# The last product of a two-layer graph kernel: four steps product by product, and eight blocks without their scale

## Chip, cores and metric

The kernel runs on one core of one Trainium2 chip. The metric is the device time of one execution in microseconds (us). All data is float32.

## What is computed

```python
def _L0_gnn_ref(cur, incidence_m):            # layer 0
    head = (incidence_m > 0).astype(float32)
    head = head / max(norm of each row of head, 1e-12)
    inc = incidence_m + head
    return (inc @ cur) / sum of each row of inc

def _L1_gnn_ref(X, A, W):                     # layer 1
    A2 = A + eye(4096)
    dscale = diagonal(A2) ** -0.5
    temp = A2 @ X @ W.T
    return relu((dscale[:, None] * A2 * dscale[None, :]) @ temp)

x = layernorm(x + _L0_gnn_ref(x, adj))        # called x1 here
x = layernorm(x + _L1_gnn_ref(x, adj, W))     # eps = 1e-5
```

x is 4096x512, adj 4096x4096, W 512x512. Row block b is rows 128b to 128b+127; there are 32. The end of the kernel computes, for each block, `layernorm(x1 + relu(dscale * C))`, where C is the block's result of the last big product and dscale one number for each row.

## The kernel before, in words

Layer 0 comes first and leaves x1 in device memory, one buffer for each row block (`x1_rows`). Then two big products follow, called k = 2 (A2 @ x1) and k = 3 (A2 @ temp, scaled). Both use a two-level scheme of seven products in place of eight. The outer level has seven products p, in the order given by `ORDER`; for k = 3 the last one is p = 4. Each outer product is done in two halves s of the columns. For each half and p there are eight steps kk = 0 to 7, and in each step the inner level makes seven matmuls, one into each of seven PSUM banks, named q1, q2, q6, q5, q7, q3, q4 (banks 0 to 6, `acc`). A matmul in float32 is two instructions on TensorE. The eighth bank, 7, is the `spare()` one, which transposes go through.

The results are kept transposed: features on the partitions, rows along the free axis, in four tiles c11, c12, c21, c22 of four feature parts each. After the eight steps of an outer product, `inner` combines the seven banks (L682 to L692) and `outer` adds the result into these tiles.

The program is written out by hand in one order[...]. The main loop (L993) goes through the steps n. In step n it first loads and prepares on VectorE (DVE) what step n + 2 needs: `prepare` calls `add_up` (L166), three additions that make the four operand sums `s` (called S3, S1, S2 and S4) of a step, and `sum_b` (L253) makes the sums `ts` of two steps of the other operand. The matmuls of q6, q5, q7 and q3 read these sums; q1, q2 and q4 don't read `s`. Then come the step's seven matmuls (`multiply2`, L278), and what the queue of finished row blocks asks for.

A row block that is finished is taken up by `layer1` (L859): its four feature parts are transposed back through bank 7 (`turn_back`, L844), ScalarE (ACT) rectifies and scales it in one operation out of PSUM (`rectify`, L848), and a part `rest`, run one step later, adds x1 on DVE (L695), takes the statistics (L149, L151), has ScalarE take the root (L153), and normalises on ScalarE (L162); the store is issued from GpSimd (POOL, L873). The block's x1 rows are fetched by `fetch` (L857), a DMA issued from POOL's queue, which stands behind POOL's earlier instructions.

In the last outer product (k = 3, p = 4, the second half) there are three such ordinary blocks left and then eight blocks whose first half of features isn't ready before the very end. These eight are taken up in pairs, four items, by `layer1_first` (L876): their second half of features, complete by then, is transposed into bank 7, rectified by two ScalarE operations, and x1 is added on POOL (L887). The items come at these places: two ordinary blocks in step kk = 1, the third and the first pair in kk = 2, the second and third pair in kk = 3, the fourth pair in kk = 4, after its matmuls.

The last steps, `TAIL` of them (three: kk = 5, 6, 7), are not multiplied in the loop but in `finish` (L895), product by product: all q1, then all q2, and so on, so that the combination of the banks can run beside the matmuls. After q7 four blocks are transposed, rectified (ScalarE) and added to x1 (POOL, L922), after q4 the other four; `measure` takes the statistics, and `leave` normalises on ScalarE or DVE and stores from SP's queue (L942).

Three buffers in turn hold the sums `s` (L241), so a step's sums can be made only when the matmuls of three steps before are over.

Of the kernel before, what the change touches and what calls it, by code (L numbers as in the profile page):

```python
# [8 lines left out]
F32 = mybir.dt.float32  # L9
BF16 = mybir.dt.bfloat16  # L10
AF = mybir.ActivationFunctionType
ALU = mybir.AluOpType

P = 128
LN_EPS = 1e-5
# [11 lines left out]
def tile_adj_resnorm_d2(  # L27
# [37 lines left out]
    nc = tc.nc  # L65
    N, D = x.shape
    H = D // 2
    NB = N // P
    NP = NB // 2
# [8 lines left out]
    SW = 512  # L78
    NS = NQ * P // SW
    SB = SW // P  # L80
# [7 lines left out]
    work = ctx.enter_context(tc.tile_pool(name="work", bufs=2))  # L88
    rows = ctx.enter_context(tc.tile_pool(name="rows", bufs=1))

    def bank(m):

        return psum.tile([P, D], F32, tag=f"q{m}", name=f"q{m}")

    def spare():
        return bank(7)

    def row_tile(tag, bufs, shape=(P, D)):
        return rows.tile(list(shape), F32, tag=tag, name=tag, bufs=bufs)


    ident = const.tile([P, P], F32, name="ident")
    make_identity(nc, ident)
    eps_t = const.tile([P, 1], F32, name="eps_t")
# [7 lines left out]
    dscale = const.tile([P, NB], F32, name="dscale")  # L112
# [3 lines left out]
    x1_rows = [dram.tile([P, D], F32, name=f"x1_{b}") for b in range(NB)]  # L116
# [39 lines left out]
    def normalise(y, mv, sd):  # L156

        rs = small.tile([P, 1], F32, name="rs")
        nc.vector.reciprocal(rs, sd)
        nb = small.tile([P, 1], F32, name="nb")  # L160
        nc.vector.scalar_tensor_tensor(nb, mv[:, 0:1], -1.0, rs, op0=ALU.mult, op1=ALU.mult)
        nc.scalar.activation(y, y, AF.Identity, scale=rs, bias=nb)  # L162
# [11 lines left out]
        nc.vector.tensor_add(pair, pair, ident.unsqueeze(1).to_broadcast([P, 2, P]))  # L174


    TAIL = 3
    LA = 2
    ORDER = {2: (4, 5, 1, 6, 7, 2, 3), 3: (2, 3, 5, 1, 6, 7, 4)}

# [8 lines left out]
    steps = [(k, s, p, kk) for k in (2, 3) for s in range(NS) for p in ORDER[k] for kk in range(NQ)]  # L189
    groups = [st[:3] + (st[3] // 2,) for st in steps[::2]]  # L190
    pools = {}
# [35 lines left out]

    def prepare(n):
        k, s, p, kk = steps[n]
        for i in range(n, len(steps) if n == len(steps) - TAIL else n + 1):  # L230
            complete(i)
        a = loaded.pop(n, None)
        r = resident[kk] if k == 2 and p != 4 and p != 7 else None
        if k == 2 and p in (3, 6):
            if a is not None:
                nc.vector.tensor_add(r, r, a)
            nc.gpsimd.dma_start(out=outer_2[s, kk, S2 if p == 6 else S4], in_=r)
            a = r
        i = made["s"]
        made["s"] += 1  # L240
        sm = (work, pools["work"], work)[i % 3].tile([P, 4, SW], F32, tag="s", name="s")  # L241
        add_up(sm, a)
        if k == 2 and p in (1, 2) and kk < EARLY:
            raises.append(lambda: nc.vector.tensor_add(r, r, a))
        ready[n] = a, sm
# [55 lines left out]
    chunks, sums, slots, counts, scale, natural = {}, {}, {}, {}, {}, {}  # L301
# [186 lines left out]
    def take(h, acc):  # L488

        y = row_tile("z", 2)  # L490
        nc.scalar.copy(y[:, 0:H], acc[0][:, 0:H])
        nc.scalar.copy(y[:, H:D], acc[1][:, 0:H])
        nc.scalar.copy(deg0[:, h:h + 1], acc[0][:, H:H + 1])
        return y
# [199 lines left out]
    def add(o, y):  # L694
        nc.vector.tensor_add(o, o, y)  # L695
# [145 lines left out]
    def turn_back(ps, at, h, r, cols, fs):  # L841

        for i, d in enumerate(2 * f + e for f in fs for e in range(2)):
            nc.tensor.transpose(ps[:, at + i * P:at + (i + 1) * P], C_of[3][h][d // 2][:, 2 * r + d % 2, cols], ident)  # L844

    def rectify(o, ps, b):

        nc.scalar.activation(o, ps, AF.Relu, scale=dscale[:, b:b + 1])  # L848

    def fetch(kind, h, *items):  # L850

        for j, _, _ in items:
            b = j + h * NP
            if b not in late:
                own = kind is layer1_first
                late[b] = late["pool"].tile([P, D], F32, tag=f"y{b}" if own else "y", name="y", bufs=1 if own else 3)
                nc.gpsimd.dma_start(out=late[b], in_=x1_rows[b])  # L857

    def layer1(h, item):  # L859

# [14 lines left out]

    def layer1_first(h, *items):  # L876

        ps = spare()
        for i, (j, r, cols) in enumerate(items):
            turn_back(ps, i * H, h, r, cols, (1,))  # L880
        for i, (j, r, cols) in enumerate(items):
            b = j + h * NP
            o = late["pool"].tile([P, D], F32, name=f"o{b}")
            st = late["pool"].tile([P, 2, 6], F32, name=f"st{b}")
            rectify(o[:, H:D], ps[:, i * H:(i + 1) * H], b)
            y, late[b] = late[b], (late[b], o, st)
            nc.gpsimd.tensor_add(o[:, H:D], o[:, H:D], y[:, H:D])  # L887

        def rest():
            for j, _, _ in items:  # L890
                _, o, st = late[j + h * NP]
                nc.vector.bn_stats(st[:, 1, :], o[:, H:D])
        later.append(rest)

    def finish(h, items, acc):  # L895


        c21 = C_of[3][h][0]
        q1, q2, q6, q5, q7, q3, q4 = range(7)
        p1, p5, u2, u3 = (row_tile(t, 1) for t in ("p1", "p5", "u2", "u3"))  # L900
        w2 = row_tile("t", 1, (P, 4, H))[:, 0:2, :].rearrange("p a d -> p (a d)")
        tail = [(steps[n][3], factors(n)) for n in range(len(steps) - TAIL, len(steps))]
        stats = {}

        def multiply(m):
            for kk, f in tail:
                right, left = f[m]
                nc.tensor.matmul(acc[m], left, right, start=False, stop=(kk == NQ - 1))  # L908

        def put(i, op):  # L910
            y = row_tile("y", 2)
            op(y)
            nc.vector.tensor_sub(c21[:, i, :], y, c21[:, i, :])

        def turn(t):
            j, r, cols = items[t]
            b = j + h * NP
            ps = bank((t + 7) % 8)
            turn_back(ps, 0, h, r, cols, (0,))
            y, o, _ = late[b]  # L920
            rectify(o[:, 0:H], ps[:, 0:H], b)
            nc.gpsimd.tensor_add(o[:, 0:H], o[:, 0:H], y[:, 0:H])  # L922

        def measure(t):
            b = items[t][0] + h * NP
            _, o, st = late[b]
            nc.vector.bn_stats(st[:, 0, :], o[:, 0:H])
            mv = late["pool"].tile([P, 2], F32, name=f"mv{b}")
            nc.vector.bn_aggr(mv, st)
            sd = late["pool"].tile([P, 1], F32, name=f"sd{b}")  # L930
            nc.scalar.activation(sd, mv[:, 1:2], AF.Sqrt, bias=eps_t)
            stats[b] = mv, sd

        def leave(t, by_act):
            b = items[t][0] + h * NP
            o, (mv, sd) = late[b][1], stats[b]
            if by_act:
                normalise(o, mv, sd)
            else:
                nc.vector.reciprocal(sd, sd)  # L940
                nc.vector.tensor_scalar(o, o, mv[:, 0:1], sd, op0=ALU.subtract, op1=ALU.mult)
            nc.sync.dma_start(out=out[b * P:(b + 1) * P, :], in_=o)  # L942

        multiply(q1)
        nc.scalar.copy(p1, acc[q1])
        multiply(q2)
        put(0, lambda o: nc.vector.tensor_add(o, acc[q2], p1))
        multiply(q6)
        nc.vector.tensor_add(u2, acc[q6], p1)
        multiply(q5)  # L950
        nc.scalar.copy(p5, acc[q5])
        nc.vector.tensor_add(w2, u2, p5)
        multiply(q3)
        put(1, lambda o: nc.vector.tensor_add(o, acc[q3], w2))
        multiply(q7)
        for t in range(4):
            turn(t)
        nc.vector.tensor_add(u3, acc[q7], u2)
        put(3, lambda o: nc.vector.scalar_tensor_tensor(o, u3, -1.0, p5, op0=ALU.mult, op1=ALU.subtract))
        multiply(q4)  # L960
        measure(0)
        measure(1)
        put(2, lambda o: nc.vector.tensor_sub(o, acc[q4], u3))
        for t in range(4, 8):
            turn(t)
        measure(2)
        measure(3)
        leave(0, True)
        leave(1, False)
        leave(2, True)  # L970
        measure(4)
        leave(3, False)
        measure(5)
        leave(4, True)
        measure(6)
        leave(5, True)
        measure(7)
        leave(6, True)
        leave(7, False)

    def take_up(item):
        kind, args = item
# [10 lines left out]
    for n, (k, s, p, kk) in enumerate(steps):  # L993
# [59 lines left out]
        if n + 1 == len(steps) // 2:  # L1053

            scope.close()
            ring3 = ctx.enter_context(tc.tile_pool(name="ring3", bufs=2))
            late["pool"] = ctx.enter_context(tc.tile_pool(name="late", bufs=1))
            i = made["a"] % 4
            pools["turn"] = [ring3] * 2 + pools["turn"][i:] + pools["turn"][:i]
            made["a"] = 0  # L1060
            PF = 3
# [36 lines left out]
```

## Time and profile before

| What | Value |
|---|---|
| Time, median of three runs | 2283.88 us (2283.74 to 2288.45) |
| The profiled execution's own time | 2284.03 us |
| Its span in the profile | 2282.1 us |
| Granted TensorE clock, mean | 0.998 |
| TensorE matmul busy | 2255.1 us, 99% |
| DVE busy | 1854.4 us, 81% |
| ScalarE busy | 417.3 us, 18% |
| GpSimd busy | 383.3 us, 17% |
| DMA | 555.8 MB, mean 244 GB/s |

In the profile's lines, L12 is line 12 of the kernel before. PE is TensorE's matmuls, PEld its weight loads, DVE VectorE, ACT ScalarE, POOL GpSimd, SP SyncE; a q behind an engine is its sequencer, which issues DMAs. A line such as "2239.33 0.56 POOL L873 ... [1.18 <-ACT o L162]" gives the start, the duration, the engine, the source line, the operation with output and input, the number of instructions, and in brackets how long the engine was idle before and what ended it. Times count from the start of the span.

### The profile page before, as it was taken

To read this page: it belongs to the slowest core of one execution; us is meant where nothing else is said; L and a number is where in the kernel's file an instruction comes from. 1 tells how busy PE (TensorE), PEld (TensorE's weight loads), DVE (VectorE), ACT (ScalarE), POOL (GpSimd) and SP (SyncE) were. 2 spreads that over 40 slices of the span, in tenths; PEclk is the share of its full clock that TensorE was granted. 3 is DMA by queue.
4 is the path that set the end of the run, shared out by engine and by line. 5 is a ranking of instruction groups with operands and counts; after the bars stand their busy time and mean duration, and the time that the engine had idled before them with its cause. 6 is when DMAs were issued, how large, how long until landed. Compare 5 with 4: busy or idle time off the path is not lost.

```text
span 2282.1 us, 22004 instructions
## 1 busy us (share of the span) xinstructions
PE 2255.1 (99%) x7359; PEld 1380.3 (60%) x7359; DVE 1854.4 (81%) x2619; ACT 417.3 (18%) x991; POOL 383.3 (17%) x548
## 2 busy tenths in 40 slices
PE   8999999999999999999999999999999999999997
PEld 6888888888888844444555444555544444444443
DVE  6988988988988777788876778887666788776788
ACT  4333223332232000000222100122110011100013
POOL 0111112211111110001333300232320000100013
PEclk9999999999999999999999999999999999999999
DMA  9788777878777576575767857576785676766573
GB/s 330 274 287 262 260 233 270 272 262 270 238 240 239 187 266 259 198 283 184 270 240 227 262 209 271 191 283 261 209 256 218 220 258 241 253 238 227 209 269 117
DMA packets 155936, 555.80 MB, mean 244 GB/s; under 512 B 17920, under 2 KB 32272, under 8 KB 117424
## 3 DMA queue, kind: packets, MB, share of 16 engines
q1 hardware_dynamic: 114624, 417.38, 51.6%
q0 software_dynamic: 41200, 137.03, 18.2%
q8 instruction: 58, 0.95, 0.2%
q14 instruction: 54, 0.44, 0.1%
HBM read 434.78 MB, written 119.55 MB: 243 GB/s over the span
## 4 chain that ended last, share of the span: by engine, by line
PE 89%; DVE 5%; DMA 3%; ACT 2%; issue 1%; POOL 0%; SPq 0%; DVEq 0%; ACTq 0%
PE q L278 55%; PE q L472 27%; PE q L766 3%; PE q L485 2%; DMA nat<-adj 2%; DVE s L167 1%; PE q L908 1%; PE q L844 1%; DVE s L169 0%; ACT z L816 0%; ACT nat L332 0%; DVE a L442 0%; DVE mask L435 0%; ACT t L816 0%; DVE ts L257 0%
## 5 line engine op out<-in xcount | busy, mean ns | idle before, releaser
L278 PE MATMUL q<-s,ts 128*128 128x512 f32 x1326 | 612.2, 592 | 0.1
L472 PE MATMUL q<-b,s 128*128 128x256 f32 (+1 forms) x1920 | 454.4, 379 | 0.0
L278 PEld LDWEIGHTS q<-s,ts 128*128 128x128 f32 x1326 | 251.6, 190 | 299.1 <-issue 268.3
L167 DVE TENSOR_TENSOR s<-a 128x1024 f32<-128x1024 f32 x236 | 290.2, 1230 | 161.4 <-PE q L278 131.3
L472 PEld LDWEIGHTS q<-b,s 128*128 128x128 f32 x1920 | 363.1, 189 | 53.1 <-DVE z L510 0.5
L472 PE MATMUL q<-b,a 128*128 128x258 f32 (+1 forms) x1440 | 352.5, 380 | 0.7 <-ACT p L503 0.6
L278 PE MATMUL q<-a,tr 128*128 128x512 f32 x692 | 329.4, 592 | 1.8 <-DMA a<-adj_r 1.8
L472 PEld LDWEIGHTS q<-b,a 128*128 128x128 f32 x1440 | 272.5, 189 | 40.9 <-ACT p L503 1.5
L278 PE MATMUL q<-s,tr 128*128 128x512 f32 x442 | 225.7, 592 | 0.0
L278 PEld LDWEIGHTS q<-a,tr 128*128 128x128 f32 x692 | 129.5, 190 | 145.1 <-issue 138.9
L332 ACT ACTIVATE nat<-nat,tiny 128x512 f32<-128x512 f32 x240 | 170.9, 714 | 235.9 <-DMA nat<-adj 235.7
L278 PE MATMUL q<-a,ts 128*128 128x512 f32 x346 | 176.8, 592 | 0.0
L169 DVE TENSOR_TENSOR s<-a,s 128x512 f32<-128x512 f32 x236 | 167.7, 711 | 8.1
L170 DVE TENSOR_TENSOR s<-a,s 128x512 f32<-128x512 f32 x236 | 167.3, 709 | 8.0
L442 DVE TENSOR_TENSOR a<-a,mask 128x1024 f32<-128x1024 f32 x123 | 150.7, 1225 | 6.6 <-DVE mask L435 0.5
L435 DVE SCALAR_TENSOR_TENSOR mask<-a,sc 128x1024 f32<-128x1024 f32 (+2 forms) x129 | 154.1, 1196 | 2.1
L278 PEld LDWEIGHTS q<-s,tr 128*128 128x128 f32 x442 | 84.0, 190 | 92.1 <-issue 84.6
L684 ACT COPY p<-q 128x512 f32<-128x512 f32 x27 | 15.6, 577 | 631.5 <-PE q L278 631.5
L278 PEld LDWEIGHTS q<-a,ts 128*128 128x128 f32 x346 | 65.7, 190 | 83.0 <-issue 76.1
L425 POOL DMA_DIRECT2D oa<-sr x64 | 57.7, 902 | 283.8 <-DVE sr L416 181.6
L873 POOL DMA_DIRECT2D out<-o x24 | 13.1, 547 | 507.8 <-ACT o L162 507.8
L278 PE MATMUL q<-r,tr 128*128 128x512 f32 x192 | 92.7, 593 | 0.0
(193 smaller groups left out, 2129.4 us busy)
## 6 DMA issues: line engine op xcount, KB each, us to landing
a<-adj_r SPq DMA_DIRECT2D x112, 1024.0 KB, 6.6
a<-oa SPq DMA_DIRECT2D x80, 1024.0 KB, 5.3
nat<-adj SPq DMA_DIRECT2D x240, 256.0 KB, 7.4
a<-adj_q SPq DMA_DIRECT2D x60, 1024.0 KB, 6.2
tr<-ob SPq DMA_DIRECT2D x112, 512.0 KB, 4.0
oa<-sr POOLq DMA_DIRECT2D x64, 512.0 KB, 7.2
oa<-r POOLq DMA_DIRECT2D x32, 1024.0 KB, 9.2
y<-x POOLq DMA_DIRECT2D x64, 256.0 KB, 7.2
```

Of the source, the lines that this page charges most:

```text
L167: nc.vector.tensor_add(s[:, S3:S1 + 1, :], a[:, A11:A22 + 1, :], a[:, A21, :].unsqueeze(1).to_broadcast([P, 2, w]))
L169: nc.vector.tensor_add(s[:, S2, :], a[:, A11, :], s[:, S1, :])
L170: nc.vector.tensor_add(s[:, S4, :], a[:, A12, :], s[:, S2, :])
L278: nc.tensor.matmul(acc[m], left, right, start=(kk == 0), stop=(kk == NQ - 1))
L332: nc.scalar.activation(y, a, AF.Sign, bias=tiny, scale=2.0 ** 64, accum_out=accum)
L425: nc.gpsimd.dma_start(out=dst, in_=sr.rearrange("p m (k i) -> p (m k) i", i=P))
L435: nc.vector.scalar_tensor_tensor(m, v, 0.0, s.unsqueeze(1).to_broadcast(list(v.shape)), op0=ALU.is_gt, op1=ALU.mult)
L442: nc.vector.tensor_add(z, z, y)
L472: nc.tensor.matmul(acc[m][:, 0:w], left, b[:, right, 0:w], start=(kk == 0), stop=(kk == NP - 1))
L485: nc.tensor.matmul(y[:, 0:w], left, slots[kk][:, op, 0:w], start=(kk == 0 and left is k1), stop=(kk == NP - 1 and left is k2))
L766: nc.tensor.matmul(ps, left[:, e, :], wt[:, right, e, :], start=(e == 0), stop=(e == 1))
L844: nc.tensor.transpose(ps[:, at + i * P:at + (i + 1) * P], C_of[3][h][d // 2][:, 2 * r + d % 2, cols], ident)
```

## The change

1. `TAIL` is four instead of three: step kk = 4 is no longer multiplied in the loop, but with the last three in `finish`, product by product. The places of the four items of `layer1_first` in the loop stay, so the third and the fourth pair's transposes now follow each other on TensorE with no matmul in between. The sums of the last two steps go into c11 and c12, which are free by then.
2. The last eight blocks are not scaled by dscale. Since layernorm takes out a common factor of a row, x1 is divided by dscale instead (`root` is 1/dscale), and eps by its square (`eps_by`). The division of x1 is done on ScalarE in `layer1_first`, directly after the rectification; DVE's addition of x1 follows one step later. POOL's additions are gone. A pair of blocks shares one tile, and one ScalarE operation rectifies both.
3. In `finish`, one DVE operation rectifies two blocks out of PSUM and adds x1 (`take`). The eight blocks are in two groups of four, r = 0 and 1. For r = 1 a quarter of the features is done ahead of the last q4 product, so that only the quarter from c21's third part is left after it; that part is finished in two halves. Root, reciprocal and offset are taken for up to four blocks at once, and eps is added on DVE ahead of the root.

The core of the diff ("..." stands for lines left out):

```diff
-    TAIL = 3
+    TAIL = 4
...
-        for i in range(n, len(steps) if n == len(steps) - TAIL else n + 1):
+        for i in range(n, len(steps) if n == len(steps) - TAIL + 1 else n + 1):
...
+        if n < len(steps) - 2:
+            sm = (work, pools["work"], work)[i % 3].tile([P, 4, SW], F32, tag="s", name="s")
+        else:
+            sm = C_of[3][0][n - len(steps) + 2]
...  fetch: one tile of two blocks
+        if kind is layer1_first:
+            late[b] = late["pool"].tile([P, 2, D], F32, name=f"y{b}")
+            for i in range(2):
+                nc.gpsimd.dma_start(out=late[b][:, i, :], in_=x1_rows[b + i])
...  layer1_first
-            rectify(o[:, H:D], ps[:, i * H:(i + 1) * H], b)
-            nc.gpsimd.tensor_add(o[:, H:D], o[:, H:D], y[:, H:D])
+        nc.scalar.activation(o[:, :, H:D], ps.rearrange("p (i d) -> p i d", i=2), AF.Relu)
+        y, late[b] = late[b], (late[b], o)
+        for i in range(2):
+            nc.scalar.activation(y[:, i, :], y[:, i, :], AF.Copy, scale=late["root"][:, b + i:b + i + 1])
         def rest():
-                nc.vector.bn_stats(st[:, 1, :], o[:, H:D])
+            add(o[:, :, H:D], y[:, :, H:D])
+            w = H // (1 + r)
+            for i in range(2):
+                for p in range(H // w, D // w):
+                    nc.vector.bn_stats(st[:, j % SB + i, p, :], o[:, i, p * w:(p + 1) * w])
...  finish, new helpers
+        def take(r, n, f, ps):
+            y, o = rows_of(r, n)
+            nc.vector.scalar_tensor_tensor(o[:, :, f], ps, 0.0, y[:, :, f], op0=ALU.max, op1=ALU.add)
+        def deviation(r, lo, hi):
+            for n in range(lo, hi):
+                nc.vector.bn_aggr(mean[r][:, n, :], late["st", r][:, n])
+            nc.vector.tensor_add(dev[r][:, lo:hi], mean[r][:, lo:hi, 1], late["eps"][:, ...])
+            nc.scalar.activation(dev[r][:, lo:hi], dev[r][:, lo:hi], AF.Sqrt)
+        def invert(r, lo, hi):
+            nc.vector.reciprocal(dev[r][:, lo:hi], dev[r][:, lo:hi])
+            nc.vector.scalar_tensor_tensor(off[r][:, lo:hi], mean[r][:, lo:hi, 0], -1.0, dev[r][:, lo:hi], ...)
...  finish, the order of the work
         multiply(q1)
         nc.scalar.copy(p1, acc[q1])
+        nc.vector.tensor_sub(e0, p1, c21[:, 0, :])
         multiply(q2)
+        nc.vector.tensor_add(c21[:, 0, :], acc[q2], e0)
         multiply(q6)
         nc.vector.tensor_add(u2, acc[q6], p1)
+        add(c21[:, 2, :], u2)
         multiply(q5)
         nc.scalar.copy(p5, acc[q5])
+        add(u2, p5)
+        nc.vector.tensor_sub(e1, u2, c21[:, 1, :])
+        add(c21[:, 3, :], u2)
         multiply(q3)
+        nc.vector.tensor_add(c21[:, 1, :], acc[q3], e1)
+        multiply(q7, slice(0, 1))
+        ...  r = 0: eight transposes into banks 7 and 0, a take for each bank
+        multiply(q7, slice(1, TAIL))
+        ...  statistics of r = 0; c21's fourth part, and its third but for q4; deviation(0, 0, 4)
+        multiply(q4, slice(0, TAIL - 1))
+        ...  r = 1: four transposes of the fourth part into bank 1, two takes
+        invert(0, 0, 4)
+        for n in range(4):
+            leave(0, n, True)
+        multiply(q4, slice(TAIL - 1, TAIL))
+        for n in (0, 2):
+            cols = slice(n * P, (n + 2) * P)
+            nc.vector.tensor_sub(c21[:, 2, cols], acc[q4][:, cols], c21[:, 2, cols])
+        for n in (0, 2):
+            ...  two transposes into bank 2 or 3, two statistics, one take
+        ...  the last statistics; deviation, invert and leave by two blocks
```

More of the change, by code (lines that the diff above doesn't have):

```diff
@@ L240, in prepare @@
         made["s"] += 1
-        sm = (work, pools["work"], work)[i % 3].tile([P, 4, SW], F32, tag="s", name="s")
+        if n < len(steps) - 2:
+            sm = (work, pools["work"], work)[i % 3].tile([P, 4, SW], F32, tag="s", name="s")
+        else:
+            sm = C_of[3][0][n - len(steps) + 2]
         add_up(sm, a)
@@ L850, in fetch @@
     def fetch(kind, h, *items):
[L852 to L857, printed above, removed]
+        b = items[0][0] + h * NP
+        if b in late:
+            return
+        if kind is layer1_first:
+            late[b] = late["pool"].tile([P, 2, D], F32, name=f"y{b}")
+            for i in range(2):
+                nc.gpsimd.dma_start(out=late[b][:, i, :], in_=x1_rows[b + i])
+        else:
+            late[b] = late["pool"].tile([P, D], F32, tag="y", name="y", bufs=3)
+            nc.gpsimd.dma_start(out=late[b], in_=x1_rows[b])
     def layer1(h, item):
@@ L880, in layer1_first @@
             turn_back(ps, i * H, h, r, cols, (1,))
[L881 to L884, printed above, removed]
-            rectify(o[:, H:D], ps[:, i * H:(i + 1) * H], b)
-            y, late[b] = late[b], (late[b], o, st)
-            nc.gpsimd.tensor_add(o[:, H:D], o[:, H:D], y[:, H:D])
-        def rest():
-            for j, _, _ in items:
-                _, o, st = late[j + h * NP]
-                nc.vector.bn_stats(st[:, 1, :], o[:, H:D])
+        j, r, _ = items[0]
+        b = j + h * NP
+        if ("st", r) not in late:
+            late["st", r] = late["pool"].tile([P, 4, 2 + 2 * r, 6], F32, name=f"st{r}")
+        st = late["st", r]
+        o = late["pool"].tile([P, 2, D], F32, name=f"o{b}")
+        nc.scalar.activation(o[:, :, H:D], ps.rearrange("p (i d) -> p i d", i=2), AF.Relu)
+        y, late[b] = late[b], (late[b], o)
+        for i in range(2):
+            nc.scalar.activation(y[:, i, :], y[:, i, :], AF.Copy, scale=late["root"][:, b + i:b + i + 1])
+        def rest():
+            add(o[:, :, H:D], y[:, :, H:D])
[3 more added lines that the diff above has]
+                    nc.vector.bn_stats(st[:, j % SB + i, p, :], o[:, i, p * w:(p + 1) * w])
         later.append(rest)
@@ L899, in finish @@
         q1, q2, q6, q5, q7, q3, q4 = range(7)
-        p1, p5, u2, u3 = (row_tile(t, 1) for t in ("p1", "p5", "u2", "u3"))
-        w2 = row_tile("t", 1, (P, 4, H))[:, 0:2, :].rearrange("p a d -> p (a d)")
+        p1, p5, u2 = (row_tile(t, 1) for t in ("p1", "p5", "u2"))
+        e0, e1 = row_tile("y", 2), row_tile("y", 2)
         tail = [(steps[n][3], factors(n)) for n in range(len(steps) - TAIL, len(steps))]
-        stats = {}
-        def multiply(m):
-            for kk, f in tail:
+        first = [items[r * SB][0] + h * NP for r in range(2)]
@@ L907, in multiply @@
+        mean, dev, off = ([late["pool"].tile([P, 4, 2] if n == "mv" else [P, 4], F32, name=f"{n}{r}") for r in range(2)]
+                          for n in ("mv", "sd", "nb"))
+        def multiply(m, of=slice(0, TAIL)):
+            for kk, f in tail[of]:
                 right, left = f[m]
                 nc.tensor.matmul(acc[m], left, right, start=False, stop=(kk == NQ - 1))
[L910 to L932, printed above, removed]
@@ L934, in leave, with turn, rows_of, measure @@
-        def leave(t, by_act):
-            b = items[t][0] + h * NP
-            o, (mv, sd) = late[b][1], stats[b]
+        def turn(r, n, i, o):
+            nc.tensor.transpose(o, c21[:, 2 * r + i, n * P:(n + 1) * P], ident)
+        def rows_of(r, n):
+            return late[first[r] + n]
+        def take(r, n, f, ps):
+            y, o = rows_of(r, n)
+            nc.vector.scalar_tensor_tensor(o[:, :, f], ps, 0.0, y[:, :, f], op0=ALU.max, op1=ALU.add)
+        def measure(r, n, i, w):
+            nc.vector.bn_stats(late["st", r][:, n, i, :], rows_of(r, n // 2 * 2)[1][:, n % 2, i * w:(i + 1) * w])
@@ new lines, in deviation @@
+        def deviation(r, lo, hi):
+            for n in range(lo, hi):
+                nc.vector.bn_aggr(mean[r][:, n, :], late["st", r][:, n])
+            nc.vector.tensor_add(dev[r][:, lo:hi], mean[r][:, lo:hi, 1], late["eps"][:, first[r] + lo:first[r] + hi])
+            nc.scalar.activation(dev[r][:, lo:hi], dev[r][:, lo:hi], AF.Sqrt)
+        def invert(r, lo, hi):
+            nc.vector.reciprocal(dev[r][:, lo:hi], dev[r][:, lo:hi])
+            nc.vector.scalar_tensor_tensor(off[r][:, lo:hi], mean[r][:, lo:hi, 0], -1.0, dev[r][:, lo:hi],
+                                           op0=ALU.mult, op1=ALU.mult)
@@ L937, in leave @@
+        def leave(r, n, by_act):
+            o = rows_of(r, n // 2 * 2)[1][:, n % 2, :]
+            rs = dev[r][:, n:n + 1]
             if by_act:
-                normalise(o, mv, sd)
+                nc.scalar.activation(o, o, AF.Identity, scale=rs, bias=off[r][:, n:n + 1])
             else:
-                nc.vector.reciprocal(sd, sd)
-                nc.vector.tensor_scalar(o, o, mv[:, 0:1], sd, op0=ALU.subtract, op1=ALU.mult)
+                nc.vector.tensor_scalar(o, o, mean[r][:, n, 0:1], rs, op0=ALU.subtract, op1=ALU.mult)
+            b = first[r] + n
@@ L945, in finish @@
         nc.scalar.copy(p1, acc[q1])
+        nc.vector.tensor_sub(e0, p1, c21[:, 0, :])
         multiply(q2)
-        put(0, lambda o: nc.vector.tensor_add(o, acc[q2], p1))
+        nc.vector.tensor_add(c21[:, 0, :], acc[q2], e0)
         multiply(q6)
         nc.vector.tensor_add(u2, acc[q6], p1)
+        add(c21[:, 2, :], u2)
         multiply(q5)
         nc.scalar.copy(p5, acc[q5])
-        nc.vector.tensor_add(w2, u2, p5)
+        add(u2, p5)
+        nc.vector.tensor_sub(e1, u2, c21[:, 1, :])
@@ L953, in finish @@
+        add(c21[:, 3, :], u2)
         multiply(q3)
[L954 to L979, printed above, removed]
+        nc.vector.tensor_add(c21[:, 1, :], acc[q3], e1)
+        multiply(q7, slice(0, 1))
+        for n in (0, 2):
+            ps = bank((7, 0)[n // 2]).rearrange("p (i d) -> p i d", i=2)
+            for i in range(2):
+                for e in range(2):
+                    turn(0, n + i, e, ps[:, i, e * P:(e + 1) * P])
+            take(0, n, slice(0, H), ps)
@@ new lines, in finish @@
+        multiply(q7, slice(1, TAIL))
+        for n in range(2):
+            measure(0, n, 0, H)
+        nc.vector.scalar_tensor_tensor(c21[:, 3, :], acc[q7], -1.0, c21[:, 3, :], op0=ALU.mult, op1=ALU.subtract)
+        nc.vector.tensor_add(c21[:, 2, :], c21[:, 2, :], acc[q7])
+        for n in range(2, 4):
+            measure(0, n, 0, H)
+        deviation(0, 0, 4)
+        multiply(q4, slice(0, TAIL - 1))
+        ps = bank(1).rearrange("p (n d) -> p n d", n=4)
+        for n in range(4):
+            turn(1, n, 1, ps[:, n, :])
@@ new lines, in finish @@
+        for n in (0, 2):
+            take(1, n, slice(P, H), ps[:, n:n + 2, :])
+        invert(0, 0, 4)
+        for n in range(4):
+            leave(0, n, True)
+        multiply(q4, slice(TAIL - 1, TAIL))
+        for n in (0, 2):
+            cols = slice(n * P, (n + 2) * P)
+            nc.vector.tensor_sub(c21[:, 2, cols], acc[q4][:, cols], c21[:, 2, cols])
+        for n in (0, 2):
+            ps = bank((2, 3)[n // 2]).rearrange("p (n d) -> p n d", n=4)
+            for i in range(2):
+                turn(1, n + i, 0, ps[:, i, :])
+                measure(1, n + i, 1, P)
+            take(1, n, slice(0, P), ps[:, 0:2, :])
@@ L981, in take_up @@
+        for n in range(2):
+            measure(1, n, 0, P)
+        deviation(1, 0, 2)
+        for n in range(2, 4):
+            measure(1, n, 0, P)
+        invert(1, 0, 2)
+        leave(1, 0, True)
+        deviation(1, 2, 4)
+        leave(1, 1, False)
+        invert(1, 2, 4)
+        leave(1, 2, True)
+        leave(1, 3, False)
     def take_up(item):
@@ L1057, in tile_adj_resnorm_d2 @@
             late["pool"] = ctx.enter_context(tc.tile_pool(name="late", bufs=1))
+            root, eps_by = (late["pool"].tile([P, NB], F32, name=t) for t in ("root", "eps_by"))
+            nc.vector.reciprocal(root, dscale)
+            nc.vector.scalar_tensor_tensor(eps_by, root, LN_EPS, root, op0=ALU.mult, op1=ALU.mult)
+            late["root"], late["eps"] = root, eps_by
             i = made["a"] % 4
```

## The prediction

> **What bounds the kernel now.** I read the page first (engine shares, chain), then the chain in order of time over the last 100 us, then the time lines of each engine there.
>
> ```profile
> PE 2255.1 (99%) x7359; PEld 1380.3 (60%) x7359; DVE 1854.4 (81%) x2619; ACT 417.3 (18%) x991; POOL 383.3 (17%) x548
> PE 89%; DVE 5%; DMA 3%; ACT 2%; issue 1%; POOL 0%; SPq 0%; DVEq 0%; ACTq 0%
> ```
>
> TensorE sets the time. Only where it stands still, above all after its last product, is there time to win. The chain near the end (start, us, what):
>
> ```profile
> 2243.04 6.01 PE q L278 x14
> 2249.05 0.44 PE q L844 x4
> 2249.49 15.45 PE q L908 x36
> 2264.94 0.23 PE q L844 x2
> ...
> 2275.61 0.76 ACT o L162
> 2276.36 0.15 issue
> 2276.51 0.65 ACT o L162
> ```
>
> One step is 14 instructions (each product is two) in 6.01 us: 0.429 us an instruction, 0.859 us a product. TensorE never stops up to the last q4 product at 2268.4; from there the chain runs over DVE, ACT and POOL to the last store, issued on SP at 2278.7, and the span's end at 2282.1. So 10.3 us from the last product to the last issue, then 3.4 us that stay. The change works on those 10.3 us, and reorders what comes before. What comes before decides, and it shows in GpSimd's time line, and below it in three rows of the time line of all engines (start, us, instruction, count, in brackets the idle time before and what ended it):
>
> ```profile
> 2239.33 0.56 POOL L873 DMA_DIRECT2D out<-o  x1 [1.18 <-ACT o L162]
> 2241.60 0.55 POOL L873 DMA_DIRECT2D out<-o  x1 [1.71 <-ACT o L162]
> 2242.13 2.13 POOL L857 DMA_DIRECT2D y<-x  x4
> 2246.22 4.72 POOL L887 TENSOR_TENSOR o<-o,y 128x256 f32<-128x256 f32 x4 [1.96 <-DMA y<-x]
> ```
>
> ```profile
> 2241.21 0.82 ACT L848 ACTIVATE o<-q,dscale 128x256 f32<-128x256 f32 x2
> ...
> 2242.08 0.14 PEld L844 LDWEIGHTS q<-ident,c 128*128 128x128 f32 x1 [0.31 <-ACT o L848]
> ...
> 2248.89 0.60 PE L844 MATMUL q<-ident,c 128*128 128x128 f32 x4
> ```
>
> I call the last eight blocks, in pairs, F1 to F4, and the last three ordinary blocks A6 to A8. The x1 rows of F2 and F3 are requested at 2242.13, because their request stands on POOL behind the stores of A6 and A7; they land 4.1 us later (2246.22). Today only POOL waits for them. And F3's transposes wait (0.31) until ScalarE has emptied bank 7 of F2: all F blocks go through that one bank.
>
> [...]a request ready long before stands behind a store, and TensorE waits for the bank although matmuls for the next step are ready. The forecast rests on this. [...]the last product ends at 2268.4 and the granted clock is 0.52 in the window 2271.5 to 2272.0, in spite of 1 us of transposes between. How long fp32 products stay slow no row shows[...].
>
> **The change, part by part** (each start below from the rows above and the durations named).
>
> *1. x1 divided on ScalarE.* Each F pair loses two 128x256 rectifications (0.82 to 0.84 together) and gets one 128x512 (0.69, row L848) and two 128x512 copies with a scale, 0.72 each (row L816, 128x512). These copies wait for the x1 rows, and in ScalarE's order they stand ahead of the next pair's rectification. F1's rows were fetched at 2214, so its copies only make ScalarE later: A6's root comes at 2238.1 (before 2237.50), A7's normalisation ends at 2241.95 (before 2241.30). A7's store and the four requests behind it on POOL move with it: first request 2242.8, rows at 2242.8 + 4.1 = 2246.9. F2's rectification ends 2242.56, F3's transposes start 2242.7 (+0.27).
>
> *2. Four steps product by product.* Step 4's 14 instructions (6.01 us) stood between F3's and F4's transposes: 2242.88 to 2248.89. They go into the tail, so F4's transposes follow F3's directly and want bank 7 at 2243.15. It is freed by F3's rectification, behind F2's copies: 2246.9 + 2 x 0.68 (the distance of two in a row) = 2248.2, + 0.69 = 2248.9, + 0.15 to the first transpose = 2249.05. **TensorE idles 5.9 us**, what the moved step used to cover.
>
> *3. DVE behind it.* A8's root (ScalarE) stands behind F2's and F3's copies: 2250.1 instead of 2245.6. DVE, in order, waits in A8's reciprocal from 2246.4 to 2250.4. Queued behind are, by rows L167 to L170, L257 to L259 and L892: A8's offset 0.3; F1's add and statistics 1.4; step 6's sums 2.6; group sums 1.5; F2's add and statistics 1.4; F3's add 0.6 and four 128-wide statistics (no row: 256 wide takes 0.41, 512 wide 0.69, so 0.29, 0.21 apart) 0.9; then step 7's S2, 1.95: ready 2261.15. POOL's adds are gone and with them their slowing of DVE (L169 took 1.10 beside them, else 0.69); I use 0.69 throughout. The adds that DVE takes over, 4 x 0.6, are in the list.
>
> *4. The tail on TensorE.* F4's transposes 0.44, then q1, q2 four times and q6 three times: 11 x 0.859 = 9.45, to 2258.9. The fourth q6 product needs step 7's S2: start 2261.3, **2.4 us idle**. Then 10 products (8.6), 0.2 waiting for c21's second part, eight transposes and restart 0.9, six products 5.15, four transposes 0.44, the last q4 product 0.86: 2277.4 instead of 2268.4. That is +9.0 = 0.27 + 5.9 + 2.4 + four more transposes ahead of the last product (0.44). The same number of products is done. [...]F4's own rows come at 2256.1 and hold p1's copy until 2258.0; DVE gets there only at 2263.4, so it costs nothing. p5's copy and DVE's eight steps up to c21's second part keep pace with q5 and q3.
>
> *5. After the last product.* Gone: one full PSUM operation and its second pass (1.35), eight transposes less four, four rectifications and four POOL adds (0.45 + 0.74 each, in a row), four of eight normalisations. Left, mostly on DVE: two half subtractions (0.34 apart), eight 128-wide statistics (0.21 apart), two rectify-and-add 128x256 (0.42; nearest row L959, 0.69 at 512), four aggregations (0.24; L929 0.21), small ones of 0.16, one root on ScalarE (0.29), the second root behind a ScalarE normalisation (0.81), last issue 0.4 later. Strung together: halves done 2278.5, both pairs added 2280.0, first root 2281.0, second 2282.5, last store issued 2284.75, 7.35 after the last product: **2.95 less** than 10.3. The first four blocks' stores go out between 2279 and 2281, under this. If rectify-and-add costs 1.10 instead of 0.69 at 512 wide, it adds 0.5; not less than 0.64 (L963), so no gain to speak of.
>
> *6. At nothing.* root and eps_by, two operations on 128x32 at mid-kernel: DVE has slack there. SP loads end at 2229. Step 6 and 7's sums in c11/c12: read last by A8's transposes at 2232.
>
> **Sum.** +9.0 - 2.95 = +6.05. The profiled execution took 2284.03 (span 2282.1), so 2290.1; it lies 0.15 over the median of 2283.88, so the forecast is 2289.9. A measurement tells 0.2%, 4.6 us, from no change.
>
> **Rivals.**
> (a) The above, 2288 to 2291.5: 0.60. For it: 2246.22, and the 0.31 wait.
> (b) The same, with a slow clock outlasting the 2.4 us cover, or a still later landing (the rows show up to 4.6 us) and DVE slowed: 2291.5 to 2295: 0.13.
> (c) The rows come in time (an earlier request): F4's transposes still wait 1.8 us for the bank and F3's copies, and the fourth q6 product still waits 2.8 us for DVE, whose deadline moved 3.4 us forward: +2.4, 2286.3: 0.17. Against it: the place of L857 on POOL.
> (d) Other side: neither stall, because bank 7 comes free at once and DVE holds step 7's S2 before TensorE asks. Then only 0.6 us of transposes against -2.95: 2281.5: 0.08. It decides if F2's rows are there by 2242 and S2 by 2255.3; today S2 comes at 2255.6 with less work ahead of it. Against it: both.
> (e) A longer stay at half clock with the stall also in q6: beyond 2295, 0.02.
>
> Slower by over 0.2% (past 2288.4): most of (a), (b), (e): 0.71. Within: (c), (d), the low edge of (a): 0.27. Faster: 0.02, since even (d) wins only 0.1%. The range runs from (c)'s upper edge, 2286.8, to 2293.0.
>
> **What would show it.** Right: an idle of 5 to 6 us on TensorE before the last L844 of the F blocks, released by ScalarE, ScalarE released by DMA y<-x, a granted clock of 0.5 about there; DVE waiting 4 us for L153; a wait of a q6 product for DVE; last product near 2277, 7 to 8 us from there to the last store's issue. Wrong: F4's transposes within 2 us of F3's (then (c) or (d)), or a tail after the last product of 10 us again.

## The result, and the profile after

| | before | after |
|---|---|---|
| Median of 19 runs each, us | 2285.07 | 2289.19 |
| Ratio after / before | | 1.0016 (95% interval 1.001 to 1.0022) |
| Profiled execution, its own time / span, us | 2284.03 / 2282.1 | 2290.79 / 2289.0 |
| A8's transposes to the span's end, us | 50.4 (from 2231.68) | 54.3 (from 2234.68) |

The change made the kernel slower, by 3.7 us of 2285 (2.3 to 5.0). That is just under the 0.2% that I had called the limit of a measurement; with 19 runs a side it is told clearly from nothing. Executions of one kernel differ by several us, and the profiled execution of after is 3.0 us late before the change begins: waits in layer 0 (L476 of after for p and s: 2.5 us; the same line before, L472: 0.6) and a TensorE clock at half after the longest of them, from 125.4 to 128.8. So from here on I compare the stretch from A8's transposes to the end of the span. It grew by 3.9 us, close to the medians' 4.1.

The page's first and fourth part, after:

```profile
PE 2259.3 (99%) x7359; PEld 1384.8 (60%) x7359; DVE 1855.5 (81%) x2635; ACT 417.7 (18%) x983; POOL 367.2 (16%) x532
PE 88%; DVE 5%; DMA 4%; ACT 2%; issue 1%; SPq 0%; DVEq 0%; POOL 0%; ACTq 0%
```

The shares hardly show it; DMA's share of the chain rose from 3% to 4%, and that is the place. The time line, all engines (line numbers are now after's: L862 is the request of the rows, L881 the store, L896 the rectification, L899 the division of x1, L848 the transposes, L926 the last products):

```profile
2242.72 0.55 POOL L881 DMA_DIRECT2D out<-o  x1 [24.36 <-ACT o L162]
2244.61 0.58 ACT L896 ACTIVATE o<-q 128x512 f32<-128x512 f32 x1
2244.99 0.55 POOL L881 DMA_DIRECT2D out<-o  x1 [1.73 <-ACT o L162]
2245.44 0.60 PE L848 MATMUL q<-ident,c 128*128 128x128 f32 x4
2245.53 2.13 POOL L862 DMA_DIRECT2D y<-x  x4
2248.86 1.39 ACT L899 ACTIVATE y<-y,root 128x512 f32<-128x512 f32 x2 [3.67 <-DMA y<-x]
2250.16 0.58 ACT L896 ACTIVATE o<-q 128x512 f32<-128x512 f32 x1
2250.78 1.11 PE L848 MATMUL q<-ident,c 128*128 128x128 f32 x4 [4.75 <-ACT o L896]
2252.17 0.17 DVE L159 RECIPROCAL rs<-sd 128x1 f32<-128x1 f32 x1 [3.18 <-ACT sd L153]
```

Read it from the fourth line on. F3's transposes are done, and F4's are next on TensorE, but bank 7 holds F3. ScalarE has F3's rectification (2250.16) behind F2's two divisions (2248.86), these wait 3.67 us for the rows, and the rows were requested only at 2245.53, behind A7's store. TensorE waits 4.75 us. DVE waits 3.18 us in A8's reciprocal, since A8's root stands on ScalarE behind all this.

The windows show the second part. Each row gives start:end, the length, the busy us of PE, PEld, DVE, ACT and POOL, then the granted clock, which is the share of its full clock that TensorE is given, and last the DMA's busy share and GB/s:

```profile
2247.00:2248.00 1.00, 0.00 (x0) 0.00 (x0) 1.00 (x2) 0.00 (x0) 0.66 (x2) 1.00 0.79 176
2249.00:2250.00 1.00, 0.00 (x0) 0.00 (x0) 0.00 (x0) 1.00 (x2) 0.00 (x0) 0.50 0.94 356
2253.00:2254.00 1.00, 1.00 (x2) 0.34 (x1) 0.97 (x4) 0.86 (x2) 0.33 (x1) 0.50 0.00 0
2256.00:2257.00 1.00, 1.00 (x4) 0.44 (x3) 1.00 (x2) 0.00 (x0) 0.00 (x0) 1.00 0.71 270
```

In this idle the clock fell to half (0.50) and stayed there 4.5 us into the new work. The sixteen instructions of q1 and q2 take from 2251.69 to 2260.37, 8.68 us instead of 16 x 0.429 = 6.87, and F4's transposes 0.91 instead of 0.44. Together 2.3 us lost.

And the end did get shorter: from the last product's end to the start of the last store's issue it is 6.5 us after (2279.05 to 2285.54), and was 10.3 before (2268.39 to 2278.66). The rows are before's and then after's:

```profile
2265.65 2.74 PE L908 MATMUL q<-a,ts 128*128 128x512 f32 x6
2278.66 0.37 SPq L942 DMA_DIRECT2D out<-o  x1
2278.03 1.02 PE L926 MATMUL q<-a,ts 128*128 128x512 f32 x2
2285.54 0.41 SPq L962 DMA_DIRECT2D out<-o  x1
```

### The profile page after: what moved, and what is told of

Same layout as the page of the kernel before. It is cut to its first block, busy times and chain, and to the rows that moved or that the text cites. A ratio compares the mean times of both kernels' runs of the same rounds, so it can differ in the third digit from the quotient of the medians.

```text
span 2289.0 us, 21981 instructions
## 1 busy us (share of the span) xinstructions
PE 2259.3 (99%) x7359; PEld 1384.8 (60%) x7359; DVE 1855.5 (81%) x2635; ACT 417.7 (18%) x983; POOL 367.2 (16%) x532
## 4 chain that ended last, share of the span: by engine, by line
PE 88%; DVE 5%; DMA 4%; ACT 2%; issue 1%; SPq 0%; DVEq 0%; POOL 0%; ACTq 0%
PE q L282 52%; PE q L476 31%; PE q L770 3%; DMA b<-x 1%; DMA nat<-adj 1%; PE q L926 1%; DVE s L167 1%; DMA a<-adj_r 1%; DVE s L169 1%; PE q L848 1%; DVE ts L261 0%; ACT z L820 0%; ACT nat L336 0%; ACT t L820 0%; DMA a<-adj_q 0%
## 5 line engine op out<-in xcount | busy, mean ns | idle before, releaser
L476 PE MATMUL q<-b,s 128*128 128x256 f32 (+1 forms) x1920 | 455.3, 380 | 0.5 <-DVE s L169 0.5
L476 PEld LDWEIGHTS q<-b,s 128*128 128x128 f32 x1920 | 364.5, 190 | 53.4 <-DVE s L169 0.9
L476 PE MATMUL q<-b,a 128*128 128x258 f32 (+1 forms) x1440 | 352.9, 381 | 2.0 <-ACT p L507 2.0
L476 PEld LDWEIGHTS q<-b,a 128*128 128x128 f32 x1440 | 273.5, 190 | 41.2 <-ACT p L507 2.4
L881 POOL DMA_DIRECT2D out<-o x24 | 13.1, 545 | 536.6 <-ACT o L162 536.6
```

The costliest lines, as they stand in the source:

```text
L476: nc.tensor.matmul(acc[m][:, 0:w], left, b[:, right, 0:w], start=(kk == 0), stop=(kk == NP - 1))
```

## The experiments

All times in us. "Stretch" is A8's transposes to the span's end in the profiled execution; "end" is the last product's end to the start of the last store's issue. Both, the waits and the clock come from one profiled execution of each kernel; the ratio comes from 13 to 22 executions of it, against executions of before taken with them. Stretch and ratio agree within 1.1 us in every row, so a difference of stretch below that rests on the traces alone.

| Kernel | Stretch | TensorE waits: bank 7 / q6 for sums / c21's second part | Half clock ahead of the end | End | Ratio to before (95%) |
|---|---|---|---|---|---|
| before | 50.4 | 0 / 0 / 0 | no | 10.3 | 1 |
| after | 54.3 | 4.75 / 0 / 0 | yes | 6.5 | 1.0016 (1.001 to 1.0022) |
| early rows | 52.9 | 0.91 / 2.94 / 0 | yes | 6.5 | 1.001 (1.0002 to 1.0018) |
| three steps | 53.0 | 0 / 3.64 / 0 | yes | 6.7 | 1.0016 (1.0009 to 1.0022) |
| sums first | 54.0 | 5.10 / 0 / 0 | yes | 6.5 | 1.0016 (1.0008 to 1.0023) |
| before, four steps | 53.2 | 0.93 / 1.68 / 0 | no | 10.0 | 1.0012 (1.0004 to 1.002) |
| three steps, early rows, sums first | 48.9 | 0 / 0 / 1.32 | no | 6.7 | 0.9991 (0.9982 to 0.9999) |
| four steps, early rows, sums first | 50.3 | 0.91 / 0.3 / 1.58 | no | 6.5 | 1.0004 (0.9996 to 1.0012) |
| three steps, sums first | 53.5 | 0 / 1.00 / 3.31 | yes | 6.7 | 1.0016 (1.0008 to 1.0023) |
| three steps, early rows, sums first, roots split | 47.4 | 0 / 0 / 0 | no | 6.7 | 0.9987 (0.9981 to 0.9993) |
| the same, additions on POOL | 47.5 | 0 / 0 / 0 | no | 6.8 | 0.9984 (0.9978 to 0.9991) |

**Early rows.** All rows of the four pairs are requested in step kk = 1, ahead of A6's and A7's stores.

```diff
-            for kind, args in queue[:2]:
+            for kind, args in queue if end else queue[:2]:
                 fetch(kind, *args)
```

> The changed kernel, with all x1 rows of the four pairs requested in step kk = 1, ahead of the stores of A6 and A7 on POOL. I count the stretch from A8's transposes to the span's end: 50.4 us before, 54.3 after the change. Theory (the rows' wait holds ScalarE, ScalarE holds bank 7): TensorE's idle before F4's transposes falls from 4.8 to about 1.4 us, ScalarE's 3.7 us waits for the rows are gone, the clock stays at 1.00; a wait of about 3 us for step 7's sums shows at the fourth q6 product in its place. Stretch about 51.5, time about 2.8 us below the changed kernel, 1 above before. Rival (the idle comes from the moved step alone, whatever the rows do): idle stays over 3 us, time within 0.5 us of the changed kernel.

The waits of its TensorE, from A8 on (total, times, longest):

```profile
PE q L926 <- DVE c L169: 2.9, 1, 2.9
PE q L848 <- ACT o L896: 0.9, 1, 0.9
PE q L930 <- DVE c L1008: 0.6, 1, 0.6
```

The bank's wait fell from 4.75 to 0.9, and ScalarE waits for no rows: the rows' lateness is shown to be the cause of that idle. The 2.9 us for step 7's sums came in its place, as expected. Not expected: even this shorter gap lowers the clock. The rows are the next instructions in TensorE's time line, and the clock in two windows:

```profile
2254.17 2.08 PE L926 MATMUL q<-c,ts 128*128 128x512 f32 x2 [2.94 <-DVE c L169]
2256.04 2.45 PE L926 MATMUL q<-s,ts 128*128 128x512 f32 x4
2258.32 1.88 PE L926 MATMUL q<-c,ts 128*128 128x512 f32 x4
...
2250.50:2254.20 3.70, 0.76 (x3) 0.03 (x1) 3.60 (x9) 0.00 (x0) 0.00 (x0) 0.94 0.00 0
2255.20:2256.20 1.00, 1.00 (x3) 0.48 (x2) 0.96 (x5) 0.00 (x0) 0.00 (x0) 0.50 0.00 0
```

The six instructions from 2254.17 take 4.15 us instead of 2.57. These 1.6 us are why the stretch is above the expected 51.5. The executions' times don't tell this kernel from the changed one (1.001 and 1.0016, the intervals overlap), so the cause of the idle is shown by the trace.

**Three steps.** `TAIL = 3`, all else as changed.

```diff
-    TAIL = 4
+    TAIL = 3
...
-        for i in range(n, len(steps) if n == len(steps) - TAIL + 1 else n + 1):
+        for i in range(n, len(steps) if n == len(steps) - 3 else n + 1):
```

> The changed kernel with three steps product by product instead of four; all else as changed. Theory: step 4's 6 us stand between F3's and F4's transposes again and cover the rows' wait, so under 0.5 us idle there and a full clock; DVE still stands 3 us in A8's reciprocal, so the fourth-last q6 product waits about 3 us for step 7's sums; the end after the last product is 6.5 to 7 us to the last store's issue. Stretch from A8's transposes to the end about 50.8, time within 1 us of before. Rival (the four steps are the whole loss): the shorter end is won in full, stretch 47 or less, time 3.5 us or more below before.

Step 4's products cover the rows' wait, as expected, but nothing is won: DVE's 3.4 us in A8's reciprocal turn into a wait of the q6 product, and that gap lowers the clock again.

```profile
PE q L926 <- DVE c L169: 3.6, 1, 3.6
PE q L930 <- DVE c L1008: 0.8, 1, 0.8
```

The rival, that the four steps are the whole loss, falls. My own number was 2.2 us low: the wait is 0.6 longer, the half clock costs 1.7 (the four instructions from 2259.95 take 3.46 instead of 1.72). By its ratio the kernel is 3.7 us above before, where I had expected it within 1.

**Sums first.** F2's and F3's additions and statistics on DVE go behind the sums of step 7.

```diff
+        if end and kk == 4:
+            later[:0] = held
+            held = []
         for rest in held:
             rest()
```

> The changed kernel with DVE's additions and statistics of F2 and F3 put behind the sums of step 7 (they came ahead of them). Step 7's sums come about 2.9 us earlier. Theory: TensorE didn't wait for them after the change, because the half clock from the idle had slowed its first products by 2.2 us; the idle of 4.8 us and the slow clock stay, so the time stays within 0.5 us of the changed kernel and the stretch at 54. Rival (DVE's order is what delays TensorE): 2 us or more below the changed kernel.

54.0 against 54.3: as expected. The gap is a little longer (5.10 us for 4.75) and the slow stretch after it shorter (the sixteen instructions of q1 and q2 take 8.06 us for 8.68), and the two nearly cancel. After the change no wait for the sums is left to be taken away; the slow clock had taken its place.

**Before, with four steps alone.** The kernel before with `TAIL = 4`, and the last two steps' sums in c11 and c12.

> The kernel before with only one part of the change: four steps product by product (with the last two steps' sums in c11 and c12); scales, POOL's additions and the end as before. Theory: ScalarE doesn't wait for rows here, so F4's transposes wait only for F3's two rectifications, about 0.9 us; the fourth q6 product waits about 2 us for step 7's sums, whose deadline is 3.4 us nearer. Stretch about 53.3, time about 2.9 us above before, clock full. Rival (the moved step costs nothing by itself, all comes from the rows): stretch 50.5, time as before.

53.2, as expected, and TensorE's row shows both waits; the q6 one:

```profile
2259.53 1.12 PE L911 MATMUL q<-c,ts 128*128 128x512 f32 x2 [1.68 <-DVE c L169]
2260.49 1.88 PE L911 MATMUL q<-s,ts 128*128 128x512 f32 x4
```

So the four steps cost 2.8 us without any division of x1. The end stays at 10.0 us: it is not the four steps that shorten it. And the clock stayed at 1.00 behind the gap of 1.7 us.

**Everything mended, with three and with four steps; and three steps with late rows.** The edits are those above, put together.

> The changed kernel with three steps product by product, the x1 rows of the four pairs requested in step kk = 1, and F2's and F3's additions and statistics behind step 7's sums. Theory: every wait that the experiments so far showed is gone (bank 7, step 7's sums, half clock), and what is left is the shorter end, 13.7 us before and 10.0 after the change from the last product to the span's end, less 0.5 us for four more transposes ahead of it. Stretch from A8's transposes to the end 47.2 us (before 50.4), time about 3.2 us below before. Rival (the end's gain depends on what had been delayed ahead of it): the end after the last product grows back, stretch over 49.

> The changed kernel, four steps kept, with the rows requested in step kk = 1 and F2's and F3's additions behind step 7's sums. Theory: bank 7 still costs 0.9 us, step 7's sums come just in time, so no 2.9 us wait and no half clock. Stretch 48.4, time about 2 us below before and 1.2 above the kernel with three steps. Rival (four steps product by product are worth something of their own): stretch below the three-step kernel's.

> As the three-step kernel with the additions behind step 7's sums, but the rows requested late, as in the changed kernel. Theory: no idle at F4's transposes, since step 4's products cover the rows' wait; DVE still stands 3.4 us in A8's reciprocal, so step 7's sums come 0.8 us late; that is too short for the clock to fall. Stretch 48.4, time about 2 us below before. Rival (late rows cost as much with three steps): stretch over 50.

Three steps with all three edits beat the kernel before: 48.9, ratio 0.9991. I expected 47.2. The end itself did not grow back (6.7 us), so the rival falls, but a wait came up that I hadn't counted:

```profile
PE q L930 <- DVE c L978: 1.3, 1, 1.3
```

c21's second part, which the first transposes of the end need, is now late on DVE. The additions put behind the sums still had to be done, and they are ahead of it. With four steps the same wait is 1.6 us, step 7's sums still come 0.3 us late, and bank 7 costs the expected 0.9, so the stretch is 50.3, 1.9 above my number; the order, three steps better than four, is as expected. The third run shows my worst miss, 53.5 for 48.4: with late rows DVE loses its 3.6 us in A8's reciprocal whatever the order, and putting work off only moved the wait, from 3.64 us at q6 to 1.0 there and 3.3 at c21's second part. Behind the gap of 1.0 us the clock stayed at 1.00, as it had behind that of 1.7 us in before with four steps; behind the 3.3 us it is at half (0.50) again. With three steps late rows do cost as much as with four, by way of DVE.

**Roots split, and POOL's additions back.** DVE is what is short from A8 on. It also stands 1.5 us in reciprocals that wait for ScalarE's roots, so blocks taken up together make all their statistics first:

```diff
-            normalise(o, mv, sd)
-            nc.gpsimd.dma_start(out=out[b * P:(b + 1) * P, :], in_=o)
+            def leave():
+                normalise(o, mv, sd)
+                nc.gpsimd.dma_start(out=out[b * P:(b + 1) * P, :], in_=o)
+            return leave
...
-        for rest in held:
-            rest()
+        for leave in [rest() for rest in held]:
+            if leave is not None:
+                leave()
```

> The three-step kernel with early rows and the additions behind step 7's sums, in which the transposes after the first q7 product waited 1.3 us for DVE. Now the statistics of the blocks taken up together are made before the first reciprocal, so that DVE doesn't wait for ScalarE's roots (1.5 us in that kernel from A6 on). Theory: DVE's total work from A8 on is what bounds this kernel once TensorE has no other wait; 1.5 us less of waiting on DVE takes the 1.3 us wait away. Stretch 47.5 (48.9 without it, 50.4 before), time about 2.9 us below before. Rival (the end of the kernel, not DVE's order, sets it): stretch stays within 0.3 of 48.9.

> The same, with the additions of x1 to the second halves of the eight blocks back on POOL, as before the change. Theory: DVE loses four operations of 0.69 (2.8 us) and is slowed beside POOL's additions by about 1.7 us, as in the kernel before, so it comes 1 us earlier; with TensorE already without a wait this is worth 0 to 0.5 us: stretch 47 to 47.5. Rival (POOL's slowing of DVE is worth more than the work taken off it): stretch 48 or more.

47.4 and 47.5, both as expected. The gain of the roots split over the kernel without it, 1.5 us, shows in the stretch; the ratios, 0.9991 and 0.9987, were taken apart from each other and their intervals overlap. The waits of the first of them, TensorE then DVE, from A8 on:

```profile
PE q L933 <- DVE c L1011: 0.8, 1, 0.8
DVE o L941 <- PE q L933: 0.6, 1, 0.6
DVE c L993 <- PE q L929: 0.2, 1, 0.2
```

One wait is left on TensorE, behind the last product, where it belongs to the end. This version is 0.13% faster than before (0.07 to 0.19%), 3 us. POOL's additions change nothing that can be told: DVE is rid of four operations, but two of the others, which take 0.69 alone, take 1.64 and 1.77 beside POOL's additions (2242.15 to 2243.90 and 2250.85 to 2252.65):

```profile
2242.68 1.77 DVE L699 TENSOR_TENSOR o<-o,y 128x512 f32<-128x512 f32 x1
2251.56 1.64 DVE L169 TENSOR_TENSOR c<-a,c 128x512 f32<-128x512 f32 x1
```

## Why the prediction was right, and where its sizes were off

Sign and range held, and so did the mechanism in its main part; the size, 6.05 us for 3.7, was too large, and the wait at q6 did not show as a wait. Counted from the forecast's base, 2283.88, a change of 3.7 us is 2287.6. That lies between (c), 2286.3, and (a), from 2288 on, and within the 0.2%, an outcome that was given 0.27. So the time alone would not have told (a) from (c); the idle in the trace and early rows do.

Of the signs that were named, the releasers, the half clock and DVE's wait for L153 are there. The idle (4.75 us for 5 to 6), the last product (2276.05 for 2277) and the end (6.5 us for 7 to 8) came out smaller, and no q6 product waits for DVE. Times of after are put 3.0 us earlier here, so that A8's transposes coincide with before.

1. *Rows divided on ScalarE.* The place was right, the durations high. The rectification without a scale takes 0.58 to 0.60, not 0.69, so F3's transposes are not late at all (0.27 forecast). Nor had they waited before: the 0.31 us that I read as a wait for bank 7 is the idle of a weight load, and 0.24 of it stands ahead of nearly every load; the transposes start at 2242.44, just 0.86 us, two instructions, after the start of the products ahead of them. The first request came at 2242.5 (2242.8 forecast), and the rows were there for ScalarE 3.3 us later, not 4.1: the largest single part of the error.
2. *The idle on TensorE.* 4.75 to 4.9 us for 5.9, by the two items above. Early rows showed its cause.
3. *DVE behind it.* It waited 3.2 us in A8's reciprocal, 4.0 forecast; step 7's S2 came at 2259.75, 2261.15 forecast.
4. *The wait at q6 and the clock.* Forecast: a 2.4 us wait, with the half clock hidden in it, whose length was an estimate that no row of before shows. Found: no wait, and 2.3 us lost to the half clock. One covers the other. At full clock the fourth q6 product would have been reached at 2247.78 + 0.44 + 11 x 0.859 = 2257.67, and step 7's S2 came at 2259.75; that is an estimated wait of 2.1 us, so the half clock added only some 0.2. The sum was right, and so, nearly, was putting nothing into it for the clock, but what TensorE spent the time on was named wrongly. In early rows the clock did cost, 1.6 us, where a gap of 2.9 us ended on it. The gaps and the half clock found behind each stand in the last section. Rows of float32 products at half clock, of which before had none, are here too: 0.85 us an instruction for 0.43. Last product: +7.7 us instead of +9.0 (4.9 idle and restart, 2.3 clock, 0.44 transposes).
5. *The end.* 3.8 us shorter, 2.95 forecast. Two 128-wide statistics take 0.47 together, the root of two columns 0.20 for my 0.29, and the last root waited about 0.25 us behind a normalisation, not 0.81. Some 0.3 us of the 0.85 had been won when the second root was done, the rest between it and the last issue (1.7 us, 2.25 forecast). All kernels with the new end have 6.5 to 6.8 us, whatever comes before, so it stands by itself. 7.7 - 3.8 = 3.9, the change of the stretch.

The rivals: (c), rows in time, was priced at +2.4; early rows has +2.5 in the stretch. That agreement is luck: the bank's wait was 0.9 smaller and the end 0.85 shorter than priced, and the clock, which was not priced, took 1.6. (d), no stall anywhere and faster, needed more than I had said: not only early rows and early sums, also fewer waits on DVE, and three steps. (b) and (e) did not occur. What carried the forecast stands in after's rows: POOL's request came only at 2245.53, behind A7's store, and ScalarE's rectification only at 2250.16, behind divisions that had waited 3.67 us for the rows.

What stays open: each kernel has one profiled execution, so how often the clock falls in a gap of 2 to 3 us over many executions is not shown, nor on what it depends.

## What to carry to other kernels

An operation that is moved to an idle engine brings its waits with it: ask what stands behind it there and who needs that, here a PSUM bank, a root, and through them TensorE and DVE. Before work that lay between two uses of one bank is moved away, price the second use without that cover. When the bound engine's waits are taken away one at a time, the next one can appear at once, as it did here three times; find which engine's total is short (here DVE's), and take waits off that engine rather than reordering its work.

## What the runs showed of the hardware that I had not expected

Whether the granted clock was at half behind a gap between TensorE's instructions, and for how long, did not go by the gap's length alone. The gaps, shortest first; the last column is the time at a granted clock of 0.50, reckoned from the windows around the gap:

| Kernel, start of the gap | Gap, us | Half clock behind its start, us |
|---|---|---|
| before, four steps, 2257.85 | 1.68 | none |
| after, 123.24 | 2.03 | 3.4 |
| three steps, 832.73 | 2.12 | none |
| early rows, 2251.23 | 2.94 | 3.4 |
| after, 2246.04 | 4.75 | 6.8 |
| sums first, 2244.52 | 5.10 | 3.4 |

The gaps from 123 and from 832 us lie far ahead of the change. The two side by side, each with the window that holds the gap's end and the next one, after's and then those of three steps:

```profile
122.01:125.42 3.41, 1.38 (x7) 0.90 (x6) 0.17 (x1) 1.27 (x4) 0.00 (x0) 1.00 1.02 393
125.42:128.83 3.41, 3.41 (x9) 2.62 (x10) 3.10 (x10) 3.35 (x10) 0.00 (x0) 0.50 0.87 297
833.10:836.51 3.41, 1.66 (x4) 0.68 (x4) 1.58 (x2) 0.00 (x0) 0.00 (x0) 1.00 1.02 416
836.51:839.92 3.41, 3.34 (x8) 1.44 (x8) 3.31 (x5) 0.00 (x0) 0.00 (x0) 1.00 1.02 425
```

Behind the gap of 2.03 us the clock was 0.50; behind that of 2.12 us it stayed at 1.00. And the gap of 4.75 us had 6.8 us at half clock, the longer one of 5.10 us only 3.4. What decided this is not shown. At half clock a float32 instruction, 512 wide, took 0.85 us for its 0.43.
